# An LSTM feeding a binarised feed-forward block: x Wx in the cell's layout, seeded into the gates' PSUM by ScalarE, the output gate in its own bank

## The chip, the cores and the metric

The kernel runs on one core of one Trainium2 chip. Time is device microseconds for one execution. The times before are 329.32, 329.71 and 330.16 us (median 329.71). Names used below: PE is TensorE (matmuls), DVE is VectorE, ACT is ScalarE, POOL is GpSimd, SP is SyncE, which only issues DMAs here. SBUF is the on-chip memory, PSUM the accumulator memory that PE writes, made of eight banks.

## The reference

For a batch of N = 32 sequences of T = 64 steps and width D = 256:

```python
xW = einsum('ntd,dg->ntg', x, Wx) + b            # Wx: 256 x 1024 (4 gates of 256)
def step(h, c, xw_t):                            # 64 times, each needs the last h
    a = xw_t + h @ Wh                            # Wh: 256 x 1024
    i, f, o = sigmoid(a[:, :256]), sigmoid(a[:, 256:512]), sigmoid(a[:, 512:768])
    g = tanh(a[:, 768:])
    c = f * c + i * g
    h = o * tanh(c)
# feed-forward on all h, with weights of +1/-1 from boolean matrices
y = concat([h, -h]); y = relu(s0 * (y @ k0)) * 2     # 512 -> 1024
y = relu(s1 * (y @ k1)) * 2                          # 1024 -> 1024
out = x + s2 * (y @ k2)                              # 1024 -> 256
```

All is fp32. The recurrence is serial over 64 steps; the feed-forward part (FFN below) can start on the first sixteen steps once they exist.

## The kernel before, in words

**Layout.** The cell works on 128 partitions that hold four quarters q of the hidden width, 32 batch rows each: partition q*32+n, free dimension 64 columns per gate. A step's gates are 256 columns there. `gates_from_h` (L275) makes them with 2 x 4 fp32 matmuls, stationary h transposed (32 columns) and moving Wh (256 columns); each of the four q writes its own 32 partitions, so four matmuls run side by side in four column groups of PE. An fp32 matmul appears as two matmul records in the trace, hence 16 per step.

**The cell.** `cell_step`: DVE adds the x part out of SBUF (`a`, L287), ACT takes the sigmoid of three gates (`sig`, L292) and the tanh of the fourth (`cand`, L294), DVE forms `kept` (L298), `new` (L300) and `c` (L302), ACT takes `th` = tanh(c) (L304), DVE forms `h` (L306) and transposes it into `hist` (L311), from which the next step's matmuls read. Each engine works its instructions strictly in the order in which the program issues them.

**x Wx.** `turn_x` (L202) transposes x on DVE. `x_block` computes blocks of 16 steps with Wx stationary (32 columns at a time) and x moving (8 steps x 32 rows = 256 columns), L219. The result has gates on partitions and must be turned: ACT evicts it with the bias (`xb`, L241) and DVE transposes it (`xg`, L238). Block 0 is computed whole before step 0.

**FFN.** After every four steps `split_h` makes `hhi` and `hlo` (L324, L325) out of hist, a high and a low part of h. `ffn_block` works on blocks of 16 steps: layer 0 (L377), layer 1 (L406), layer 2 (L391), matmuls of 128 x 128 weights and 512 columns, each layer's result evicted as a high part by ACT (L330) and a low part by DVE (L331). A block has 192 such matmuls.

**Order.** All engines' orders are written by hand. The program emits, for each step t: the gates' matmuls, the cell, then a "chore" (one piece of the FFN's weights: `make_w0` L179/L180, `make_w1` L185, `make_w2` L189), then PE filler: so many pieces of x Wx (steps 0 to 16) or of the FFN (12 matmuls per step from step 17) that PE has work while the cell runs. The 192 matmuls of the last FFN block and the rest of the third follow after step 63.

**Loads.** x (L80) and the weights come by DMA. SP issues most: x's first block and Wx (L107, L117), Wh (L120), x's second block, the booleans k0 (L136, used by `make_w0` in steps 0 to 3) and k1, k2 (`load_bits`). ACT issues a share of the first ones, POOL the bias, the initial h and the scales. The eight hardware DMA semaphores are used in turn, so an issue waits for the transfer that was issued eight before it.

Of the kernel before, what the change touches and what calls it, by code (L numbers as in the profile page):

```python
# [36 lines left out]
def lstm_ffn(ctx: ExitStack, tc: tile.TileContext, x, cond, wx_d, wh_d, b_d, k0_d, k1_d, k2_d, s0_d, s1_d, s2_d, out):  # L38
# [10 lines left out]
    NM = G // P  # L49
# [4 lines left out]
    PER_STEP = 12  # L54
    LAG = SB + 1
# [4 lines left out]
    gpool = ctx.enter_context(tc.tile_pool(name="xg", bufs=NB))  # L60
# [4 lines left out]
    ps_g = ctx.enter_context(tc.tile_pool(name="ps_g", bufs=2, space=PSUM))  # L65
# [10 lines left out]
    def load_x(i, half, engines):  # L76
        t = xq[i, half] = xpool.tile([P, SB // 2, HQ], F32, tag="x", name=f"x{i}_{half}")
        t0 = i * SB + half * (SB // 2)
        for q in range(NQ):
            engines[q % len(engines)].dma_start(  # L80
                out=t[q * N : (q + 1) * N], in_=x[:, t0 : t0 + SB // 2, ts(q, HQ)]
            )


    small = const.tile([P, 96], F32, name="small")
    b_raw, bias = small[:, :32], small[:, 32:64]
    nc.vector.memset(b_raw, 0.0)
    wh = const.tile([P, 2, G], F32, name="wh")
    w0 = const.tile([P, 2, F0], F32R, name="w0")
# [8 lines left out]
    wx_rows = wx_d.rearrange("(q b j) g -> q j b g", q=NQ, b=2)  # L98
    wx = [act([P, 2, H], F32, f"wx{g}") for g in range(4)]

# [3 lines left out]
    load_x(0, 0, [nc.sync, nc.scalar])  # L104
    for q in range(NQ):
        engine = (nc.sync, nc.scalar)[q % 2]
        engine.dma_start(out=rows(wx[0], q), in_=wx_rows[q, :, :, :H])  # L107
    load_x(0, 1, [nc.sync, nc.scalar])
# [3 lines left out]
    b_rows = b_d.rearrange("(g q b j) -> q g b j", g=4, q=NQ, b=2)  # L112
    for q in range(NQ):
        nc.gpsimd.dma_start(out=b_raw[q * 32 : q * 32 + NM], in_=b_rows[q])
    for g in range(1, 4):
        for q in range(NQ):
            nc.sync.dma_start(out=rows(wx[g], q), in_=wx_rows[q, :, :, ts(g, H)])  # L117
    wh_rows = wh_d.rearrange("(q b j) g -> q j b g", q=NQ, b=2)
    for q in range(NQ):
        nc.sync.dma_start(out=rows(wh, q), in_=wh_rows[q])  # L120
# [55 lines left out]
    def make_w0(k, half):  # L176
# [3 lines left out]
        nc.vector.scalar_tensor_tensor(  # L180
# [19 lines left out]
    def turn_x(i, half):  # L200
        full = act([P, SB // 2, 2, N], F32, f"xT{i}_{half}")
        nc.vector.transpose(  # L202
            full.rearrange("p t b n -> p (t b n)"), xq[i, half].rearrange("p t j -> p (t j)")
        )
        xT[i, half] = full

    xg = {}

    def x_block(i):
        xg[i] = gpool.tile([P, SB, G // NQ], F32, tag="xg", name=f"xg{i}")  # L210

        for m0, side in ((0, 2), *((m, 1) for m in range(2, NM))) if i == 0 else ((m, 1) for m in range(NM)):
            ps = [ps_f.tile([P, 2, SB // 2, N], F32, tag="pf", name=f"px{i}_{m0 + j}") for j in range(side)]
            for half in range(2):
                for j in range(side):
                    g, b = divmod(m0 + j, 2)
                    for k in range(2):
                        for q in range(NQ):
                            nc.tensor.matmul(  # L219
                                ps[j][q * 32 : (q + 1) * 32, half],  # L220
                                wx[g][:, k, ts(2 * q + b, 32)],
                                xT[i, half][:, :, k, :],
                                start=(k == 0),
                                stop=(k == 1),
                                skip_group_check=True,
                            )
                        if k == 0:
                            yield 2
                    if half:
                        finish_x(i, m0 + j, ps[j])  # L230
                    yield 2

    def finish_x(i, m, p):
        out_t = xg[i]
        tmp = act([P, TB], F32, f"xb{i}_{m}")

        def turn(out_t=out_t, m=m, tmp=tmp):
            nc.vector.transpose(out_t[:, :, ts(m, 32)], tmp.rearrange("p (t n) -> p t n", n=N))  # L238

        def add_bias(m=m, p=p, tmp=tmp, turn=turn):  # L240
            nc.scalar.activation(  # L241
                tmp, p.rearrange("p h t n -> p (h t n)"), AF.Identity, bias=bias[:, m : m + 1]
            )
            on_vector(turn)

        on_scalar(add_bias)

    vector_queue, scalar_queue = deque(), deque()  # L250
    late = [False]

    def on_vector(f):
        vector_queue.append(f)

    def on_scalar(f):
        if late[0]:
            scalar_queue.append(f)
        else:
            f()  # L260

    def flush_vector(n=None):
        while vector_queue and n != 0:
            vector_queue.popleft()()
            n = None if n is None else n - 1


    wh_q = wh.rearrange("p k (g q j) -> p k q g j", g=4, q=NQ)
    hist, hparts = {}, {}
# [15 lines left out]
    def cell_step(t, g, c):  # L285
# [9 lines left out]
        while scalar_queue:  # L295
            scalar_queue.popleft()()
# [151 lines left out]
    n = 0  # L448
# [84 lines left out]
```

## Time and profile before

| What | us |
|---|---|
| Median of three runs | 329.71 |
| Profiled execution, its own time | 329.05 |
| Its span, first to last instruction | 327.2 |
| First gates (step 0) begin | 20.7 |
| Gates of step 2 begin | 29.52 |
| Gates of step 17 begin | 86.82 |
| Gates of step 63 begin | 270.14 |
| Last FFN block begins | 277.50 |
| Last matmul begins | 320.93 |

The span is the time between the first and the last instruction; 1.85 us of the execution lie around it. "Busy" is time in which an engine has an instruction in work; a matmul's end is modelled, so starts are the better guide on PE. In a row of the timeline the columns are start, duration, engine, line, operation, output<-inputs, shape, count, and in brackets the idle time before and what ended it. In the waits, the columns are total us, times, longest us.

### The profile page before, as it was taken

Reading aid. Unit: us, or ns where it says so; the run is one execution under the profiler, and the core shown is the slowest. Engines: PE = TensorE matmul, PEld = TensorE weight load, DVE = VectorE, ACT = ScalarE, POOL = GpSimd, SP = SyncE. Lnnn points to the kernel's source line nnn. Section 1 sums busy time; section 2 is a strip of 40 time slices with the busy share of each in tenths; the row PEclk is TensorE's granted clock in tenths of the full one; section 3 lists DMA queues with packets and bytes.
Section 4 is the critical chain, followed back from the end, with each engine's and each line's share of the span. In section 5 each row is a group of like instructions: output and inputs, shape, how many; then the busy total and the mean of one; then the engine's idle time right before and its main releaser. Section 6 shows DMA issues by size and latency. Waiting matters only on the chain.

```text
span 327.2 us, 7012 instructions
## 1 busy us (share of the span) xinstructions
PE 312.0 (95%) x2825; PEld 207.3 (63%) x2825; DVE 174.5 (53%) x538; ACT 125.5 (38%) x324; POOL 9.0 (3%) x27
## 2 busy tenths in 40 slices
PE   7987898999999999999999999999999999999992
PEld 3645555656666666666666666666666666888881
DVE  2357766665685445446856454568564444811104
ACT  1434566756653523234523232335232322511111
POOL 6200000000000000000000000000000000000001
PEclk9999999999999999999999999999999999999997
DMA  5765200104100000000010300000110000130002
GB/s 135 181 141 144 54 19 18 34 18 109 42 2 0 3 0 0 2 2 1 0 34 8 90 1 2 0 3 0 32 34 0 2 0 3 47 81 2 0 0 65
DMA packets 30864, 10.72 MB, mean 33 GB/s; under 512 B 28008, under 2 KB 30568, under 8 KB 30832
## 3 DMA queue, kind: packets, MB, share of 16 engines
q1 hardware_dynamic: 28224, 9.58, 12.4%
q10 hardware_dynamic: 2336, 0.66, 0.9%
q8 instruction: 22, 0.36, 0.5%
q0 software_dynamic: 272, 0.04, 0.1%
q14 instruction: 10, 0.08, 0.1%
HBM read 8.16 MB, written 2.10 MB: 31 GB/s over the span
## 4 chain that ended last, share of the span: by engine, by line
PE 79%; DVE 7%; DMA 5%; ACT 3%; SPq 2%; issue 2%; ACTq 0%; DVEq 0%
PE p L406 38%; PE gates L275 18%; PE p L377 10%; PE po L391 9%; PE px L219 5%; DMA x<-in_x_dram 2%; DVE xg L238 2%; DMA wh<-in_L_cond_Wh_dram 2%; SPq L117 2%; DVE a L287 1%; DMA wx<-in_L_cond_Wx_dram 1%; ACT xb L241 1%; ACT th L304 1%; DVE xT L202 1%; DVE h L306 1%
## 5 line engine op out<-in xcount | busy, mean ns | idle before, releaser
L275 PE MATMUL gates<-wh,hist 128*32 128x256 f32 x1008 | 67.5, 385 | 6.5 <-DVE hist L311 6.0
L292 ACT ACTIVATE sig<-a 128x192 f32<-128x192 f32 x64 | 23.4, 365 | 98.1 <-DVE a L287 98.1
L219 PE MATMUL px<-xT,wx 128*32 128x256 f32 x1024 | 59.3, 379 | 0.5 <-DVE xT L202 0.5
L287 DVE TENSOR_TENSOR a<-gates,xg 128x256 f32<-128x256 f32 x64 | 27.1, 423 | 55.7 <-PE gates L275 55.4
L275 PEld LDWEIGHTS gates<-wh,hist 128*32 128x32 f32 x1008 | 27.6, 109 | 40.6 <-issue 23.3
L219 PEld LDWEIGHTS px<-xT,wx 128*32 128x32 f32 x1024 | 37.8, 110 | 18.8 <-DVE xT L202 1.8
L304 ACT ACTIVATE th<-c 128x64 f32<-128x64 f32 x64 | 16.4, 257 | 35.9 <-DVE c L302 35.7
L306 DVE TENSOR_TENSOR h<-sig,th 128x64 f32<-128x64 f32 x64 | 14.4, 225 | 24.7 <-ACT th L304 24.7
L377 PE MATMUL p<-hhi,w 128*128 128x512 f32 x64 | 26.1, 408 | 0.0
L377 PE MATMUL p<-hlo,w 128*128 128x512 f32 x64 | 25.2, 393 | 0.0
L241 ACT ACTIVATE xb<-px,small 128x512 f32<-128x512 f32 x32 | 21.6, 674 | 9.1 <-PE px L219 9.0
L238 DVE STREAM_TRANSPOSE xg<-xb 128x512 f32<-128x512 f32 x32 | 22.1, 692 | 4.0 <-ACT xb L241 3.9
L298 DVE TENSOR_TENSOR kept<-sig,c 128x64 f32<-128x64 f32 x63 | 13.2, 210 | 8.7 <-ACT sig L292 8.7
L311 DVE STREAM_TRANSPOSE hist<-h 128x64 f32<-128x64 f32 x64 | 15.7, 246 | 2.2
L377 PEld LDWEIGHTS p<-hhi,w 128*128 128x128 f32 x64 | 12.0, 187 | 6.1 <-issue 3.3
L302 DVE TENSOR_TENSOR c<-kept,new 128x64 f32<-128x64 f32 x64 | 14.4, 225 | 2.2
L294 ACT ACTIVATE cand<-a 128x64 f32<-128x64 f32 x64 | 15.4, 240 | 0.0
L300 DVE TENSOR_TENSOR new<-sig,cand 128x64 f32<-128x64 f32 x64 | 14.1, 221 | 0.0
L406 PE MATMUL p<-a_2h,w 128*128 128x512 f32 x32 | 13.9, 433 | 0.0
L377 PEld LDWEIGHTS p<-hlo,w 128*128 128x128 f32 x64 | 12.0, 188 | 2.4
L406 PE MATMUL p<-a_6h,w 128*128 128x512 f32 x32 | 13.5, 423 | 0.0
L406 PE MATMUL p<-a_4h,w 128*128 128x512 f32 x32 | 13.2, 414 | 0.0
(119 smaller groups left out, 485.6 us busy)
## 6 DMA issues: line engine op xcount, KB each, us to landing
x<-in_x_dram SPq DMA_DIRECT2D x60, 64.0 KB, 2.7
out_dram<-o SPq DMA_DIRECT2D x28, 64.0 KB, 1.8
bits<-in_L_ffn_k_dram SPq DMA_DIRECT2D x10, 128.0 KB, 2.6
wh<-in_L_cond_Wh_dram SPq DMA_DIRECT2D x4, 256.0 KB, 4.3
wx<-in_L_cond_Wx_dram SPq DMA_DIRECT2D x14, 64.0 KB, 2.7
k<-in_L_ffn_k_dram SPq DMA_DIRECT2D x8, 64.0 KB, 1.9
x<-in_x_dram ACTq DMA_DIRECT2D x4, 64.0 KB, 2.6
out_dram<-o ACTq DMA_DIRECT2D x4, 64.0 KB, 2.0
```

The costliest lines, as they stand in the source:

```text
L219: nc.tensor.matmul(ps[j][q * 32 : (q + 1) * 32, half], wx[g][:, k, ts(2 * q + b, 32)], xT[i, half][:, :, k, :], start=(k == 0), stop=(k == 1),
L238: nc.vector.transpose(out_t[:, :, ts(m, 32)], tmp.rearrange("p (t n) -> p t n", n=N))
L241: nc.scalar.activation(tmp, p.rearrange("p h t n -> p (h t n)"), AF.Identity, bias=bias[:, m : m + 1])
L275: nc.tensor.matmul(g[q * N : (q + 1) * N], hT[:, k, :], wh_q[:, k, q], start=(k == 0), stop=(k == 1), skip_group_check=True,)
L287: nc.vector.tensor_tensor(a.rearrange("p g j -> p (g j)"), g.rearrange("p g j -> p (g j)"), xg[t // SB][:, t % SB, :], ALU.add)
L292: nc.scalar.activation(sig, a[:, 0:3, :], AF.Sigmoid)
L304: nc.scalar.activation(th, c, AF.Tanh)
L306: nc.vector.tensor_mul(h, sig[:, 2, :], th)
L311: nc.vector.transpose(hT, h.rearrange("p (b j) -> p b j", b=2))
L377: nc.tensor.matmul(p, w0[:, k, ts(m, P)], a[:, k, :], start=(n == 0), stop=(n == 3))
L391: nc.tensor.matmul(po[m], w2[:, m, k], a1[k][n], start=(k == 0 and n == 0), stop=(k == FC1 - 1 and n == 1))
L406: nc.tensor.matmul(p1[m], w1[:, k, ts(m, P)], a0[k][n], start=(k == 0 and n == 0), stop=(k == FC0 - 1 and n == 1),)
```

## The change

1. **x Wx in the cell's layout.** `x_part` takes x of one step as the stationary operand (32 columns) and Wx as the moving one (256 columns, four gates of the quarter q), so that the product stands on partitions as the gates do. Two steps share a PSUM bank. DVE evicts a bank with the bias added (`evict_x`, 128 x 512); the transposes of the result (L238) and ACT's evictions (L241) are gone. The bias is loaded replicated over the batch rows.
2. **Seeding.** After `th` of step t, ACT copies the x part of step t+1 out of SBUF into the gates' PSUM; the h matmuls add to it (`start=False`). The addition `a` on DVE is gone, and the sigmoids and tanh read PSUM.
3. **Gate order and banks.** The gates stand as g, i, f in one bank (192 columns) and o in another (64 columns). The h matmuls do the first bank, then the second: 8 matmuls of 192 columns and 8 of 64 per step instead of 8 of 256. `sig` is now a sigmoid of i and f, then `cand`, then a sigmoid of o.
4. **Order.** 10 steps of x Wx are done before step 0 (before: 16), the first 8 of them in two halves of the gates. Steps 0 to 20 share PE with the rest of x Wx, steps 21 to 63 with the first three FFN blocks (576 matmuls; before: 564 from step 17). Low parts of FFN evictions are emitted on DVE right behind ACT's. The DVE half of `make_w0` follows the step's x Wx pieces.
5. **Loads.** Wx and Wh come gate by gate, on the SP and ACT queues in turn (before: after the first Wx gate and x block, on SP alone). x's third block is loaded before step 0.

```diff
-    PER_STEP = 12
-    LAG = SB + 1
+    GATES = (3, 0, 1, 2)
+    AHEAD = 10
+    X_STEPS = 21
...
+    load_x(0, 0, [nc.sync, nc.scalar], slice(0, SB // 4))
+    load_gates(wx, wx_d, (2, 3), [nc.sync, nc.scalar])
+    load_x(0, 0, [nc.sync, nc.scalar], slice(SB // 4, SB // 2))
...
+    for q in range(NQ):
+        nc.gpsimd.dma_start(out=rows(bias, q)[:, 1:], in_=b_rows[q].partition_broadcast(N))
+    nc.gpsimd.tensor_copy(bias[:, 0], bias[:, 4])
+    for slot in range(2):
+        load_gates(wx, wx_d, (slot,), [nc.sync, nc.scalar])
     load_x(0, 1, [nc.sync, nc.scalar])
-    for g in range(1, 4):
-        for q in range(NQ):
-            nc.sync.dma_start(out=rows(wx[g], q), in_=wx_rows[q, :, :, ts(g, H)])
-    for q in range(NQ):
-        nc.sync.dma_start(out=rows(wh, q), in_=wh_rows[q])
+    load_gates(wh, wh_d, (0,), [nc.sync, nc.scalar])
+    load_gates(wh, wh_d, (1, 2, 3), [nc.sync, nc.scalar])
...
+    def x_part(p, t, k, slots, start):
+        i, s = divmod(t, SB // 2)
+        for q in range(NQ):
+            nc.tensor.matmul(
+                p[q * N : (q + 1) * N, t % 2, slots],
+                xT[i // 2, i % 2][:, s, k, :],
+                wx_q[:, k, q, slots],
+                start=start, stop=False, skip_group_check=True,
+            )
+    def evict_x(p, t):
+        xg[t] = gpool.tile([P, 2, 4 * HQ], F32, tag="xg", name=f"xg{t}")
+        b = bias[:, :4].rearrange("p g j -> p (g j)").unsqueeze(1).to_broadcast([P, 2, 4 * HQ])
+        nc.vector.tensor_tensor(xg[t], p.rearrange("p t g j -> p t (g j)"), b, ALU.add)
+    def x_products(t0, t1):
+        for t in range(t0, t1, 2):
+            p = x_bank(t)
+            for s in range(2):
+                for k in range(2):
+                    x_part(p, t + s, k, slice(0, 4), s == 0 and k == 0)
+                    if s == 1 and k == 1:
+                        evict_x(p, t)
+                        half, left = divmod(t + 2, SB // 2)
+                        if left == SB // 4 and half + 1 < 2 * NB:
+                            turn_x(*divmod(half + 1, 2))
+                            if half + 5 < 2 * NB:
+                                load_x(*divmod(half + 5, 2), [nc.sync])
+                    yield 2
...
+    gates = [ps_g.tile([P, n, HQ], F32, tag=f"gates{n}", name=f"gates{n}") for n in (3, 1)]
     def gates_from_h(t, hT):
-        g = ps_g.tile([P, 4, HQ], F32, tag="gates", name=f"gates{t}")
-        for k in range(2):
-            for q in range(NQ):
-                nc.tensor.matmul(g[q * N : (q + 1) * N], hT[:, k, :], wh_q[:, k, q],
-                                 start=(k == 0), stop=(k == 1), skip_group_check=True)
+        for g, slots in zip(gates, (slice(0, 3), slice(3, 4))):
+            for k in range(2):
+                for q in range(NQ):
+                    nc.tensor.matmul(g[q * N : (q + 1) * N], hT[:, k, :], wh_q[:, k, q, slots],
+                                     start=False, stop=(k == 1), skip_group_check=True)
+    def gates_from_x(t):
+        x_t = xg[t // 2 * 2][:, t % 2].rearrange("p (g j) -> p g j", g=4)
+        nc.scalar.copy(gates[0], x_t[:, :3])
+        nc.scalar.copy(gates[1], x_t[:, 3:])
-    def cell_step(t, g, c):
-        nc.vector.tensor_tensor(a..., g..., xg[t // SB][:, t % SB, :], ALU.add)
-        nc.scalar.activation(sig, a[:, 0:3, :], AF.Sigmoid)
-        nc.scalar.activation(cand, a[:, 3, :], AF.Tanh)
+    def cell_step(t, c):
+        nc.scalar.activation(sig[:, 0:2, :], gates[0][:, 1:3], AF.Sigmoid)
+        nc.scalar.activation(cand, gates[0][:, 0], AF.Tanh)
+        nc.scalar.activation(sig[:, 2, :], gates[1][:, 0], AF.Sigmoid)
...
         nc.vector.transpose(hT, h.rearrange("p (b j) -> p b j", b=2))
+        if t + 1 < T:
+            gates_from_x(t + 1)
...
+    for slots in (slice(2, 4), slice(0, 2)):
+        for t in range(SB // 2):
+            for k in range(2):
+                x_part(banks[t // 2], t, k, slots, slots.start == 2 and t % 2 == 0 and k == 0)
+            if slots.start == 0 and t % 2:
+                evict_x(banks[t // 2], t - 1)
...
+    work = x_products(AHEAD, T)
     for t in range(T):
-        g = gates_from_h(t, hT)
-        c, hT = cell_step(t, g, c)
+        gates_from_h(t, hT)
+        c, hT = cell_step(t, c)
+        later = chores.popleft()() if chores else None
+        if t == X_STEPS:
+            work, done = ffn(), 0
+        goal = (t + 1) * total_x // X_STEPS if t < X_STEPS else (t + 1 - X_STEPS) * total_ffn // (T - X_STEPS)
         while done < goal:
             done += next(work)
+        if callable(later):
+            later()
         if t % SH == SH - 1:
             split_h(t // SH)
```

## The prediction

> **What bounds the kernel now.** I read the busy table and its slices first, then busy time by stage, then the waits of the recurrent stage, and then one step of each stage in the timeline.
>
> ```profile
> PE 312.0 (95%) x2825; PEld 207.3 (63%) x2825; DVE 174.5 (53%) x538; ACT 125.5 (38%) x324; POOL 9.0 (3%) x27
> PEclk9999999999999999999999999999999999999997
> ```
>
> TensorE (PE) is busy for 95% and its clock is full, so time is either PE work or one of PE's few gaps. The busy time of three stretches tells where the gaps are. Columns: stretch, its length, then PE, weight load, DVE, ACT and POOL busy with counts, clock, DMA share, GB/s.
>
> ```profile
> 2.00:20.70 18.70, 17.59 (x264) 9.11 (x262) 5.91 (x12) 6.88 (x10) 6.63 (x21) 1.00 0.76 171
> 20.70:86.80 66.10, 59.64 (x1040) 37.92 (x1041) 45.60 (x140) 39.54 (x92) 0.00 (x0) 1.00 0.26 62
> 86.80:270.10 183.30, 183.28 (x1288) 119.31 (x1288) 103.70 (x347) 66.90 (x201) 0.00 (x0) 1.00 0.04 10
> ```
>
> The first stretch is the start (products of 16 steps before the first gates at 20.7), the second the 17 steps that share PE with x Wx, the third the 47 steps that share it with the feed-forward part (FFN). The second idles PE for 6.5 us, the third for nothing. What PE waits for in the second, from the waits of that window:
>
> ```profile
> ACT sig L292 <- DVE a L287: 19.0, 17, 2.9
> PE gates L275 <- DVE hist L311: 6.0, 10, 1.3
> ```
>
> So there the recurrence itself, gates to hist, sets the pace. One step of it in the timeline:
>
> ```profile
> 64.34 1.07 PE L275 MATMUL gates<-wh,hist 128*32 128x256 f32 x16
> 65.20 2.80 PE L219 MATMUL px<-xT,wx 128*32 128x256 f32 x48
> ...
> 65.47 0.42 DVE L287 TENSOR_TENSOR a<-gates,xg 128x256 f32<-128x256 f32 x1 [0.68 <-PE gates L275]
> ...
> 65.99 0.36 ACT L292 ACTIVATE sig<-a 128x192 f32<-128x192 f32 x1 [0.62 <-DVE a L287]
> ...
> 66.44 0.18 DVE L298 TENSOR_TENSOR kept<-sig,c 128x64 f32<-128x64 f32 x1
> 66.54 0.22 DVE L300 TENSOR_TENSOR new<-sig,cand 128x64 f32<-128x64 f32 x1
> ...
> 67.11 0.26 ACT L304 ACTIVATE th<-c 128x64 f32<-128x64 f32 x1 [0.61 <-DVE c L302]
> ...
> 67.66 0.25 DVE L311 STREAM_TRANSPOSE hist<-h 128x64 f32<-128x64 f32 x1
> ...
> 68.05 0.42 PE L275 MATMUL gates<-wh,hist 128*32 128x256 f32 x4
> ```
>
> From gates to gates 3.71 us: 1.13 to `a`, 0.52 to `sig`, 0.55 to `new`, 1.51 to the next gates. PE needs less: 16 gate matmuls take 65.20 - 64.34 = 0.86 (53.7 ns each, streamed), 48 of px 2.58, together 3.44. In the FFN stretch it is the reverse:
>
> ```profile
> 135.93 0.40 PE L406 MATMUL p<-a_0l,w 128*128 128x512 f32 x1
> ...
> 138.26 0.39 PE L406 MATMUL p<-a_5l,w 128*128 128x512 f32 x1
> 138.57 1.07 PE L275 MATMUL gates<-wh,hist 128*32 128x256 f32 x16
> ```
>
> Ten FFN matmuls from 135.93 to 138.26 are 0.233 each; a step is 138.57 - 134.59 = 3.99, of which 12 x 0.233 = 2.79 are FFN and 1.19 gates with the switch to 32-column groups and back. The same chain of 3.7 us lies under it.
>
> **Part 1: the recurrence.** `a` on DVE goes; `sig` and `cand` read PSUM. They wait for the first bank only, three quarters of the stream: 1.13 - 0.22 = 0.91 after the gates begin (before: 1.65). `sig` now has 128 columns, about 0.31; `cand` starts 0.22 after it and takes 0.24, so `new` comes at 1.41, and the row's 1.51 follows: a chain of 2.92 instead of 3.71. The output gate's sigmoid (64 columns, 0.24) is ready by 1.13 + 0.24 or behind `cand`, at 1.6, before `th` at 1.98: hidden. The chain falls below PE's own work, so the x stage becomes PE-bound, and the FFN stretch, PE-bound already, gains nothing from it directly.
>
> Added waits: the gates now wait for two ScalarE copies. The nearest rows for them are `sig` at 192 columns (0.36) and `cand` at 64 (0.24). Queued behind `th`, the first can start 0.16 after it (as xb did, 67.27) and ends at 0.52; the second ends at 0.67. `h` and `hist` end 0.80 after `th` starts. They cover the copies by 0.13; without the cover a delay would go into the chain, whose slack is 0.12 in the x stage and 1.4 in the FFN one. Behind the copies on ACT stand the weight chores (0.71 and 1.23) and `hhi` (0.40): 2.5 + 1.23 + 0.40 = 4.1 after the gates, against the next `sig` due at 3.04 + 0.91 = 3.95; a tenth or two, in two steps.
>
> **Part 2: splitting the gates' matmuls.** 16 matmuls of 256 columns become 16 of 192 and 16 of 64. The columns streamed are the same: 16 x 40.3 + 16 x 13.4 ns = 0.86. What is unknown is the price of the short ones. The Trainium skill's page "TensorE: Matmul & The Clock Gate" (section "Wait — 56ns, not 53.3ns?") speaks against it: starts are never closer than about 25 ns however few the columns. By that the 64-column half costs 16 x 25 = 0.40 instead of 0.21, 0.19 more per step, 12 us over 64 steps, which makes the kernel slower. The trace's row differs in kind, because four column groups run side by side: in the 30 ns from 138.57 four gate matmuls start. A short fp32 matmul also occupies its group for 4 x 13.4 = 54 ns, longer than that floor, and the visible part of a first load is 24 ns (403 against 379 ns of duration in the gates' rows). Ends: 0 and 0.19; I take 0.03, near the row.
>
> **Part 3: x Wx.** Matmul count and columns stay (1024 of 256 in the whole kernel; the first eight steps in halves of 128, same stream). 32 ScalarE xb (0.67) and 32 DVE turns (0.69) go; 32 DVE evictions with the bias, 512 columns out of PSUM, come at about 0.68 (row of the FFN's a_l). ACT gains 64 x (0.36 + 0.24) of copies and 64 more sigmoids. None of it is on PE. PE's step in the x stage: 0.86 + 0.03 + 5 x 8 x 0.0537 = 3.04, or 3.47 in the three steps with six pieces. Steps 2 to 20: 16 x 3.04 + 3 x 3.47 = 59.05. DVE is first in, first out: after step 3's `hist` (2.80) stand two evictions, a turn of x, a w0 half and `hlo`, 2 x 0.68 + 0.70 + 0.74 + 0.42 = 3.2, to 6.0, while `kept` is due at 3.47 + 1.26 = 4.73; with smaller cases in four steps with a turn I add 1.7. Sum 60.75.
>
> **Part 4: the start.** Each DMA issue takes SP about 0.47 and waits for the transfer eight issues earlier. SP issues 20 loads before x's second block, then 14; ACT takes the rest. wh landed at 18.1 (four of 256 KB, 1.2 us apart); with both queues issuing I put it near 15, and PE's own work before the gates (8 halves twice, 6.9, two more steps, 1.7, waiting for half of wx at about 6 and the rest at about 9.5) also ends near 14.6. First gates: 15.3 instead of 20.7. But step 0 holds a chore: w0's first part on ACT and its second on DVE, ahead of `kept` of step 1, and both need k0:
>
> ```profile
> 10.53 2.64 SPq L120 DMA_DIRECT2D wh<-in_L_cond_Wh_dram  x4
> 13.21 5.26 SPq L80 DMA_DIRECT2D x<-in_x_dram  x8
> 18.51 4.92 SPq L136 DMA_DIRECT2D k<-in_L_ffn_k_dram  x8
> ```
>
> Its last landing was near 25.0 (issued at 23.0, 1.9 to land), just before it was used at 26.34. In the new start it would be used at 19. Six issues fewer on SP bring it 6 x 0.47 = 2.8 forward, to 22.2; at wh's rate, the 14 x 256 KB up to k0's end, counted from 2.5 us, take 16.8 and end at 19.3; no gain leaves 25.0. I take 21.6, near the issue-bound end. This is what is late next: DVE ends the w0 half at 22.35, and `kept` to the next gates is 68.05 - 66.44 = 1.61, so the gates of step 2 start at 23.95 (before 29.52), whatever PE did earlier.
>
> **Sum.** Gates of step 21: 23.95 + 60.75 = 84.7. FFN steps: 576 matmuls in 43 steps are 13.4, so 3.99 + 1.4 x 0.233 + 0.03 = 4.345; 42 of them bring the gates of step 63 to 267.2. Before, those were at 270.14 and the last FFN block began at 277.50, with 23 matmuls between; now 13 or 14 stand there: 4.35 + 0.4 for a wait on the last eviction as now, so it begins at 271.95, 5.55 earlier. The rest (192 matmuls, outputs) is unchanged. Span 327.2 - 5.55 = 321.65, its execution 329.05 - 5.55 = 323.5, and since the median shown is 0.66 above that execution, 324.2.
>
> **Rivals.** (a) *The start gains nothing*: k0 lands at 25.0 as now, gates of step 2 at 27.35: 3.4 less, 327.6. For it: DMA is busy 76% in that stretch. Against: the second issuing queue.
> (b) *Short matmuls pay a floor* (the other side): 0.19 instead of 0.03 in each of 64 PE-bound steps is 10 more, 334. It decides from 0.03 + 5.55/64 = 0.12 per step. For it: the rule; against: four starts in 30 ns.
> (c) *The chain isn't shortened*: copies or PSUM reads run late and the x stage keeps a 3.4 us pace, 19 x 0.25 = 4.8 back: 329. For it: only 0.13 of cover; against: the rows.
> (d) *More*: k0 comes at wh's rate, 2.3 earlier, and half of the DVE queueing is absorbed: 321.
>
> **How the numbers follow.** Forecast 0.60 (own range 322 to 326.5), (a) 0.14, (b) 0.13, (c) 0.07, (d) 0.06. Within 0.3%, about 1 us, is what a measurement of this kernel can't tell from no change: 0.05, nearly all from (c). Faster: 0.60 + 0.14 + 0.06 + 0.02 = 0.82; slower 0.13. The range goes from 320, inside (d), to 329, which takes in (a) and most of (c) and leaves (b) out.
>
> **What would show it.** Gates of step 0 near 15.3, a long wait of step 1's `kept` or of w0 on k0's transfer, gates of step 2 near 24; steps of about 3.05 after step 4 with PE without gaps; gates of step 21 near 84.7; FFN steps of 4.35. A gates run over 1.1 us from first start to the next matmul would prove (b); PE waiting for ACT copies, (c).

## The result, and the profile after

| Kernel | Median of its runs, us | Ratio to the kernel before | 95% interval |
|---|---|---|---|
| Before (runs beside it) | 329.51 (328.10 to 330.16) | 1 | |
| Changed | 324.85 (324.65 to 325.26) | 0.9866 | 0.9832 to 0.9900 |

The forecast was 324.2. The profiled execution of the changed kernel took 325.26, its span is 323.5 (before: 329.05 and 327.2). The total was right, but by luck: two of its terms were wrong by 3 to 5 us in opposite directions, so I go through the stages. First the busy table of the page and its clock row (PEclk, the share of TensorE's full clock that was granted, in tenths).

```profile
PE 309.4 (96%) x3979; PEld 236.8 (73%) x3979; DVE 154.0 (48%) x473; ACT 131.0 (41%) x484; POOL 9.2 (3%) x28
PEclk9997999999999999999999999999999999999998
```

PE is still the busiest engine. What is new is the 7 in the fourth slice of the clock row (24 to 32 us): PE was granted less than its full clock there, which the kernel before showed in its last slice only. The same by stage, cut at the first gates, the gates of step 2, of step 21 and of step 63 (columns as in the prediction: stretch, its length, busy time of PE, weight load, DVE, ACT and POOL, clock, DMA share, GB/s):

```profile
2.00:17.57 15.57, 14.20 (x298) 10.77 (x297) 4.30 (x9) 1.95 (x4) 6.71 (x22) 1.00 0.77 193
17.57:28.50 10.93, 6.27 (x148) 4.71 (x145) 4.92 (x15) 3.17 (x14) 0.00 (x0) 0.97 0.52 135
28.50:89.48 60.98, 60.59 (x1392) 46.12 (x1396) 41.07 (x133) 36.70 (x134) 0.00 (x0) 0.98 0.21 50
89.48:268.69 179.21, 179.21 (x1910) 135.50 (x1903) 85.34 (x281) 77.04 (x309) 0.00 (x0) 1.00 0.04 10
```

From the gates of step 2 to those of step 21 PE now idles for 0.4 us; the stretch of x Wx before, which counted steps 0 and 1 in, idled it for 6.5. After the first gates, nearly all of PE's idle time is in the second row: two steps take 10.93 us, and PE works for 6.27 of them. The timeline of that stretch shows what it waits for (brackets: idle time before, and what ended it).

```profile
12.10 6.96 SPq L84 DMA_DIRECT2D x<-in_x_dram  x8
...
19.10 5.47 SPq L146 DMA_DIRECT2D k<-in_L_ffn_k_dram  x8
...
20.59 1.08 PE L269 MATMUL gates<-wh,hist 128*32 128x192 f32 x32
...
24.34 0.72 ACT L189 ACTIVATE w0t<-k,sgn 128x512 f32<-128x512 uint8 x1 [4.22 <-DMA k<-in_L_ffn_k_dram]
...
26.25 0.75 DVE L190 SCALAR_TENSOR_TENSOR w<-k,nsgn,w0t 128x512 fp32r<-128x512 uint8 x1 [4.51 <-DMA k<-in_L_ffn_k_dram]
...
26.92 0.22 DVE L290 TENSOR_TENSOR kept<-sig,c 128x64 f32<-128x64 f32 x1
...
28.50 1.93 PE L269 MATMUL gates<-wh,hist 128*32 128x192 f32 x32 [4.67 <-DVE hist L303]
```

Read it from below: the gates of step 2 waited 4.67 us for `hist`; `hist` comes from `kept` at 26.92, which stands on DVE behind the w0 half of step 0; that half waited 4.51 us for k0, whose issues on SP began only at 19.10. The chain of the prediction is there, 4.5 us later than forecast.

One step of the x stage, to be held against the one shown before:

```profile
52.12 1.08 PE L269 MATMUL gates<-wh,hist 128*32 128x192 f32 x32
...
53.09 0.28 ACT L286 ACTIVATE sig<-gates 128x128 f32<-128x128 f32 x1
53.27 0.22 ACT L287 ACTIVATE cand<-gates 128x64 f32<-128x64 f32 x1
53.37 0.23 ACT L288 ACTIVATE sig<-gates 128x64 f32<-128x64 f32 x1
...
53.55 0.22 DVE L292 TENSOR_TENSOR new<-sig,cand 128x64 f32<-128x64 f32 x1
...
54.47 0.20 ACT L281 COPY gates<-xg 128x64 f32<-128x64 f32 x1
54.60 0.24 DVE L303 STREAM_TRANSPOSE hist<-h 128x64 f32<-128x64 f32 x1
...
55.15 0.37 PE L269 MATMUL gates<-wh,hist 128*32 128x192 f32 x4
```

A step is 3.03 us. `hist` ends at 54.84, 2.72 after the gates began, and the next gates wait for nothing but PE's own work until 55.15. The last copy ends at 54.67, 0.17 before `hist`: hidden, as forecast (0.13). In the FFN stretch:

```profile
153.34 1.08 PE L269 MATMUL gates<-wh,hist 128*32 128x192 f32 x32
154.35 0.50 PE L371 MATMUL p<-hhi,w 128*128 128x512 f32 x1
...
157.43 0.39 PE L371 MATMUL p<-hlo,w 128*128 128x512 f32 x1
157.74 1.08 PE L269 MATMUL gates<-wh,hist 128*32 128x192 f32 x32
```

The run of 32 gate matmuls takes 1.01 us to the first FFN matmul; 16 of 256 columns took 1.00 by the same measure before (medians over the FFN steps). A step with 14 FFN matmuls is 4.41, one with 13 is 4.18.

Where the 1.85 us between the forecast span (321.65) and the measured one come from:

| Stretch | Forecast, us | Measured, us | Difference |
|---|---|---|---|
| To the gates of step 2 | 23.95 | 28.50 | +4.55 |
| Gates of step 2 to 21 | 60.75 | 60.98 | +0.23 |
| Gates of step 21 to 63 | 182.5 | 179.21 | -3.3 |
| Gates of step 63 to the last FFN block | 4.75 | 4.73 | 0 |
| From there to the end | 49.7 | 50.08 | +0.4 |

### The profile page after: what moved, and what is told of

The parts are those of the page before. It is cut to its first block, busy times and chain, and to the rows that moved or that the text cites. A ratio compares the mean times of both kernels' runs of the same rounds, so it can differ in the third digit from the quotient of the medians.

```text
span 323.5 us, 9433 instructions
## 1 busy us (share of the span) xinstructions
PE 309.4 (96%) x3979; PEld 236.8 (73%) x3979; DVE 154.0 (48%) x473; ACT 131.0 (41%) x484; POOL 9.2 (3%) x28
## 4 chain that ended last, share of the span: by engine, by line
PE 87%; DMA 5%; DVE 3%; SPq 3%; issue 1%; ACT 1%; DVEq 0%; ACTq 0%
PE p L399 38%; PE gates L269 19%; PE px L226 12%; PE p L371 10%; PE po L384 9%; DMA x<-in_x_dram 2%; DMA wh<-in_L_cond_Wh_dram 2%; SPq L146 1%; SPq L84 1%; DMA k<-in_L_ffn_k_dram 1%; DMA wx<-in_L_cond_Wx_dram 1%; DVE w L190 0%; DVE xg L241 0%; ACT th L296 0%; DVE hist L303 0%
## 5 line engine op out<-in xcount | busy, mean ns | idle before, releaser
L269 PEld LDWEIGHTS gates<-wh,hist 128*32 128x32 f32 x2016 | 54.6, 110 | 30.3 <-issue 14.1
L269 PE MATMUL gates<-wh,hist 128*32 128x192 f32 x2016 | 68.9, 277 | 5.0 <-DVE hist L303 5.0
L226 PE MATMUL px<-wx,xT 128*32 128x256 f32 (+1 forms) x1152 | 62.2, 366 | 1.4 <-DMA wx<-in_L_cond_Wx_dram 1.4
L226 PEld LDWEIGHTS px<-wx,xT 128*32 128x32 f32 x1152 | 41.3, 115 | 13.8 <-issue 2.7
L286 ACT ACTIVATE sig<-gates 128x128 f32<-128x128 f32 x64 | 17.7, 277 | 82.7 <-PE gates L269 82.5
L241 DVE TENSOR_TENSOR xg<-px,bias 128x512 f32<-128x512 f32 x32 | 21.2, 666 | 5.9 <-POOL nsgn L158 4.8
L280 ACT COPY gates<-xg 128x192 f32<-128x192 f32 x64 | 20.0, 313 | 8.4 <-DVE xg L241 8.4
L288 ACT ACTIVATE sig<-gates 128x64 f32<-128x64 f32 x64 | 14.8, 231 | 0.0
L287 ACT ACTIVATE cand<-gates 128x64 f32<-128x64 f32 x64 | 14.0, 218 | 0.1
L399 PE MATMUL p<-a_7h,w 128*128 128x512 f32 x32 | 13.0, 407 | 0.0
L281 ACT COPY gates<-xg 128x64 f32<-128x64 f32 x64 | 13.0, 203 | 0.0
```

What stands on the lines that cost most here:

```text
L226: nc.tensor.matmul(p[q * N : (q + 1) * N, t % 2, slots], xT[i // 2, i % 2][:, s, k, :], wx_q[:, k, q, slots], start=start, stop=False, ski ...
L241: nc.vector.tensor_tensor(xg[t], p.rearrange("p t g j -> p t (g j)"), b, ALU.add)
L269: nc.tensor.matmul(g[q * N : (q + 1) * N], hT[:, k, :], wh_q[:, k, q, slots], start=False, stop=(k == 1), skip_group_check=True,)
L280: nc.scalar.copy(gates[0], x_t[:, :3])
L286: nc.scalar.activation(sig[:, 0:2, :], gates[0][:, 1:3], AF.Sigmoid)
L288: nc.scalar.activation(sig[:, 2, :], gates[1][:, 0], AF.Sigmoid)
```

## The experiments

The theory is that of the prediction: the time is PE's work plus PE's gaps; the recurrence no longer sets the pace, and what remains is the wait of step 1 for k0. The rivals are that the seeding or the bank of its own did not matter, that short matmuls cost a floor, and that the start's loss lies in something other than k0's place. Each kernel below is the changed kernel with one edit, the last one with three; ratios are to the kernel before, run beside it on the same chip.

### 1. The chores begin in step 3

```diff
-        later = chores.popleft()() if chores else None
+        later = chores.popleft()() if chores and t >= 3 else None
```

> The changed kernel with the weight chores starting at step 3 instead of step 0; nothing else moves. Theory (k0's transfer, through make_w0's two halves ahead of sig and kept of step 1, pins the gates of step 2 at 28.5): those gates come 2 x 3.03 after the first ones, near 23.7, PE's 4.7 us gap there is gone, and about 0.5 comes back because step 6 now has a w0 half beside two evictions and a turn: 320.5 us. Rival (the start is limited by the transfers as such, x's second block or Wh): the gap stays in another place and the time is within 1 us of 324.9.

Measured: 321.76 us, ratio 0.9776 (0.9751 to 0.9802). Its busy time in the three steps from the first gates:

```profile
18.55:27.64 9.09, 9.09 (x216) 7.27 (x220) 5.35 (x19) 3.37 (x18) 0.00 (x0) 1.00 0.55 152
```

Steps 0 to 2 take 3.03 each, PE has no gap and full clock. The gates of step 3 come at 27.64 instead of 32.83; some is given back in step 7, which takes 3.71 because the last w0 half and a turn of x stand on DVE ahead of its `kept`, so the gates of step 21 come at 84.84 instead of 89.48. The stall of step 1 was the chore's, and moving one condition by three steps brings some 3 us. (The two profiled executions lie 4.7 apart; the changed kernel's, 325.26, is the longest of its four runs, and this one's, 320.56, the second shortest of its five.)

### 2. All four gates in one bank

One bank of 256 columns, h matmuls of 256 columns again, one copy of 256; the activations wait for the whole.

```diff
-    gates = [ps_g.tile([P, n, HQ], ...) for n in (3, 1)]
+    gates = [ps_g.tile([P, 4, HQ], ...)]
-        for g, slots in zip(gates, (slice(0, 3), slice(3, 4))):
+        for g, slots in zip(gates, (slice(0, 4),)):
...
-        nc.scalar.copy(gates[0], x_t[:, :3])
-        nc.scalar.copy(gates[1], x_t[:, 3:])
+        nc.scalar.copy(gates[0], x_t)
```

> The changed kernel with the four gates in one bank again: 8 matmuls of 256 columns, one copy of 256 columns by ScalarE, all three activations wait for the whole. Theory (the split takes a quarter of the stream, 0.22 us, off a chain of 2.86 that lies just below PE's 3.03, and costs PE about 0.01 per step): x steps of about 3.08 instead of 3.03, FFN steps the same, time 325 to 326. Rival (short matmuls cost PE, a floor of 25 ns each): FFN steps 0.1 to 0.19 shorter, time 315 to 320. Rival (the output gate's own bank is a large part of the gain): slower by more than 2 us, 327 or more.

Measured: 327.21 us, ratio 0.9944 (0.9922 to 0.9966). x steps are 3.09 instead of 3.03, FFN steps 4.21 and 4.44 instead of 4.18 and 4.41:

```profile
141.36 1.07 PE L269 MATMUL gates<-wh,hist 128*32 128x256 f32 x16
142.36 0.50 PE L383 MATMUL po<-a_4h,w 128*128 128x512 f32 x1
...
145.80 1.07 PE L269 MATMUL gates<-wh,hist 128*32 128x256 f32 x16
```

The gates' run is 1.00 here and 1.01 in the changed kernel, yet the step of 14 matmuls is 4.44 against 4.41: what follows the gates is slower after matmuls of 256 columns. By position, the medians of the distances between FFN matmuls are 0.240, 0.235, 0.233 and 0.236 us for the second to fifth here, the same as in the kernel before, and 0.236, 0.228, 0.233 and 0.231 in the changed one. So splitting the gates, which I priced as a cost, pays. The 0.03 in each of 42 FFN steps, 1.3 us, was not expected; with it the time reaches the number of the second rival, though the output gate's bank makes up less than half of the 2.4 us, as the next run shows.

### 3. One bank, but the matmuls stay split

As in 2, with the h matmuls cut into 64 columns (the output gate, first) and 192.

```diff
-        for g, slots in zip(gates, (slice(0, 4),)):
+        for g, slots in ((gates[0][:, 3:4], slice(3, 4)), (gates[0][:, 0:3], slice(0, 3))):
```

> All four gates in one bank and one copy of 256 columns, as in the run with one bank, but the h matmuls stay cut: first 64 columns for o, then 192 for the other three, so that the activations wait for the last pass as there. With one bank and 256-column matmuls the FFN matmuls after the gates stood 0.235 us apart against 0.228, and the FFN steps took 4.21 and 4.44 us against 4.18 and 4.41. Theory A (it is the width of the gates' matmuls): here 0.228 again, 4.18 and 4.41, time 325.5 to 326. Theory B (it is the bank, or what ACT and PE do in it): 0.235, 4.21 and 4.44, time near 327.2. If only the last pass before the FFN counts (192 columns here, 64 in the changed kernel, 256 in the run with one bank): a value between.

Measured: 325.51 us, ratio 0.9890 (0.9869 to 0.9911). FFN steps are 4.18 and 4.41 again and the distances are those of the changed kernel: theory A. It is the cut of the gates' matmuls and not the bank, nor the order of the passes; their width and their number change together, and these runs do not part them. The bank of its own is worth the rest: x steps are 3.10 here, against 3.03. There `sig` begins 1.20 us after the gates, behind the last pass, instead of 0.97, and 0.23 on a chain of 2.88 (measured under 6) is 3.11: the chain is the longer side again.

### 4. The addition back on DVE

The copies into PSUM are left out; DVE adds the x part out of PSUM (192 and 64 columns), the activations read SBUF. Matmuls, banks and order stay.

```diff
-                        start=False,
+                        start=(k == 0),
...
+        nc.vector.tensor_tensor(a[:, :3], gates[0], x_t[:, :3], ALU.add)
+        nc.vector.tensor_tensor(a[:, 3:], gates[1], x_t[:, 3:], ALU.add)
+        # sig, cand and sig read a; gates_from_x is not called
```

> The changed kernel without the seeding: the h matmuls start their banks, DVE adds the x part out of PSUM (192 columns, then 64), the activations read SBUF, ScalarE copies nothing. Layout, banks and order stay. Theory (the shorter chain is what makes the x stage PE-bound): the chain grows by 0.45 to about 3.3, x steps go from 3.03 to about 3.35, 18 steps make 5 to 6 us, FFN steps gain nothing or lose 0.05 each: 330 to 332 us. Rival (PE's work alone sets the time, and the layout is the gain): within 1 us of 324.9.

Measured: 334.10 us, ratio 1.0160 (1.0141 to 1.0179), 2 us above the expectation and slower than the kernel before. One of its x steps:

```profile
52.48 1.08 PE L269 MATMUL gates<-wh,hist 128*32 128x192 f32 x32 [0.74 <-DVE hist L307]
...
53.69 0.35 DVE L288 TENSOR_TENSOR a<-gates,xg 128x192 f32<-128x192 f32 x1
53.95 0.21 DVE L289 TENSOR_TENSOR a<-gates,xg 128x64 f32<-128x64 f32 x1
54.13 0.31 ACT L290 ACTIVATE sig<-a 128x128 f32<-128x128 f32 x1 [0.82 <-DVE a L288]
...
56.04 1.08 PE L269 MATMUL gates<-wh,hist 128*32 128x192 f32 x32 [0.33 <-DVE hist L307]
```

`sig` begins 1.65 after the gates instead of 0.97, the step is 3.56, and PE waits for `hist` in it. Eight of the nineteen steps from 2 to 20 take 3.29 to 3.30, near the 3.35 expected; the others take up to 4.78, which the expectation missed. The gates of step 21 come at 97.41 instead of 89.48. FFN steps stay at 4.18 and 4.41, so the faster FFN steps are not owed to the seeding. The seeding is what makes the x stage PE-bound; without it this kernel loses.

### 5. The gates' matmuls cut to 64 columns

```diff
-        for g, slots in zip(gates, (slice(0, 3), slice(3, 4))):
+        for s in range(4):
+            g, slots = (gates[0][:, s : s + 1], slice(s, s + 1)) if s < 3 else (gates[1], slice(3, 4))
```

> The h matmuls of the first bank are cut once more, so that a step's gates are 64 matmul records of 64 columns instead of 16 of 192 and 16 of 64; banks, copies and activations stay. Theory (a short matmul costs its columns: the trace shows 56 ns for a pass of four records of 64 columns and 162.5 ns for four of 192): 16 passes of 56 are 0.90 us instead of 0.87, the run of gates takes 1.03 us to the next FFN weight load, and the time is 324.9 + 64 x 0.022 = 326.3 us. Rival (records start no closer than 25 ns on average): 64 starts are 1.60 us, 0.73 more in each step, and the time is near 371 us. A middle case (the twice as many weight loads cost something that is not hidden): gates of 1.1 to 1.3 us, 330 to 345 us.

Measured: 328.95 us, ratio 1.0005 (0.9983 to 1.0028). In the forms of its groups (last columns: busy time, and mean ns of one matmul, which overlap):

```profile
L270 PE MATMUL gates<-wh,hist 128*32 128x64 f32 x4032 | 72.0, 222 | 3.6 <-DVE hist L304 3.4 <-issue 0.2
```

64 short matmuls a step, and the FFN steps are 4.20 and 4.43: 0.02 more each, as the theory had it. The floor of 25 ns per start would have added 0.73 to every step. So the rule that the prediction weighed does not hold for matmuls in four column groups. The rest of the 4 us is not in the FFN stretch: the gates of step 21 come at 93.05, 3.6 later than in the changed kernel. Of these, 1.6 stand before step 2 and have nothing to do with the matmuls: the w0 half that waits for k0 began at 27.80 instead of 26.25, in a kernel with the same loads, and the gates of step 2 follow it by 2.25 in both. The other 2.0 are in the x stage, where several steps take 0.1 to 0.4 more and the weight load is idle for an issue that the profile puts down to nothing. That part was not settled.

### 6. Other splits of x Wx: 17 steps, or 16 steps ahead

```diff
-    X_STEPS = 21
+    X_STEPS = 17
```

> The changed kernel with x Wx spread over 17 steps instead of 21, and the FFN over 47 instead of 43. Theory (both stages are PE-bound, so the division of filler among steps only moves work): x steps near 3.6, FFN steps near 4.0; four more gates stand among FFN matmuls, which costs 4 x 0.32, and the stalls of steps 1 and 3 are covered by a little more filler: 324 to 325.5 us. Rival (the division is itself a source of the gain): 327 us or more.

Measured: 322.87 us, ratio 0.9820 (0.9801 to 0.9839), better than expected. The gates of step 2 come at 27.59, 0.9 earlier, because the w0 half that waits for k0 began at 25.33, 0.9 earlier than in the changed kernel's profile; the loads are the same. What the split itself did: more pieces of x Wx fall into step 1, so PE ran out 1.5 later and idled 2.26 us, not 4.67, and its clock stayed full afterwards.

```diff
-    AHEAD = 10
+    AHEAD = 16
```

> 16 steps of x Wx before the first gates instead of 10, so that PE has its work behind it while step 1 waits for k0; the loads and the chores stay. Theory (the end is PE work plus PE's gaps, and step 1's gap of 4.7 us behind k0 is what the start lost): six more steps of products (6 x 0.86 = 5.2 us) stand before the first gates, which begin near 22.7; k0 still lands near 26.1, w0 of step 1 no longer waits for long, gates of step 2 near 28.9, but 24 pieces fewer are left for steps 2 to 20, which take 2.6 to 3.0 us instead of 3.03 to 3.6: 321.5 us. Rival 1 (the steps of the x stage are held by the recurrence's chain at 2.9 us or more, so that fewer pieces do not shorten them): gates of step 21 at 86 or later instead of 89.5, time 322 to 323.5. Rival 2 (the products before the first gates only push everything back): 326 to 330.

Measured: 320.22 us, ratio 0.9750 (0.9723 to 0.9777). The first gates come at 21.36, those of step 2 at 27.27, without any stall: PE had its work while k0 was under way. Steps of five pieces take 3.03, most steps of four 2.88:

```profile
30.45 1.08 PE L269 MATMUL gates<-wh,hist 128*32 128x192 f32 x32
...
32.93 0.24 DVE L303 STREAM_TRANSPOSE hist<-h 128x64 f32<-128x64 f32 x1
...
33.29 0.51 PEld L269 LDWEIGHTS gates<-wh,hist 128*32 128x32 f32 x16 [0.52 <-ACT gates L281]
```

With four pieces PE needs 0.87 + 4 x 0.43 = 2.6, so 2.88 is the recurrence's own pace: this run measures the chain that the prediction put at 2.92. (The last row names the second copy, L281, as what ended the wait; it ended at 33.00, and `hist`, which the weight load reads, at 33.17.)

### 7. Where k0's loads stand

First, k0's eight loads on SP ahead of x's second block instead of behind it.

```diff
-    load_x(1, 0, [nc.sync])
-    load_x(1, 1, [nc.sync])
...
         k0_bits.append(t)
+    load_x(1, 0, [nc.sync])
+    load_x(1, 1, [nc.sync])
```

> On SP k0's eight loads stand before x's second block instead of behind it. Theory (SP's place in the queue sets both): k0's issues run from 12.1 to about 19 and land by 20.7; x's second block takes k0's old place and its first half lands near 22.6; in step 0 DVE has the turn of that half ahead of w0 and of the kept of step 1, so the stall does not go but moves: turn to 23.3, w0 to 24.0, gates of step 2 near 25.7, time 324.9 - 2.8 = 322.1 us. Rival (bytes, not the place in the queue): k0 lands at 24 or later whatever its place, gates of step 2 near 28, time 324.5 to 326.

Measured: 322.70 us, ratio 0.9806 (0.9773 to 0.9839).

```profile
20.43 0.72 ACT L189 ACTIVATE w0t<-k,sgn 128x512 f32<-128x512 uint8 x1
...
23.60 0.71 DVE L213 STREAM_TRANSPOSE xT<-x 128x512 f32<-128x512 f32 x1 [2.11 <-DMA x<-in_x_dram]
24.24 0.71 DVE L190 SCALAR_TENSOR_TENSOR w<-k,nsgn,w0t 128x512 fp32r<-128x512 uint8 x1
...
26.45 1.93 PE L269 MATMUL gates<-wh,hist 128*32 128x192 f32 x32 [2.25 <-DVE hist L303]
```

k0 is there by 20.4, and now the turn of x's second block waits, on the same DVE, ahead of the same `kept`: the stall moves and halves, as the theory said (gates of step 2 at 26.45, expected 25.7). Of the six runs, three with a mean clock of 0.996 to 0.998 took 321.29 to 321.88 us, the other three, at 0.988 to 0.992, took 323.52 to 324.30; the profile is of the second kind, with half clock after the stall. Then, k0's loads issued by POOL:

```diff
-            nc.sync.dma_start(out=rows(t, q), in_=k0_rows[i, q])
+            nc.gpsimd.dma_start(out=rows(t, q), in_=k0_rows[i, q])
```

> k0's eight loads are issued by POOL behind its scales (free from 10.6 us on) instead of by SP behind x's second block; everything else stays. Theory (k0 came at 26.1 because SP reached it only at 19.1, its issues waiting for older transfers, not because the DMA engines were full): eight issues of 0.55 us from 10.6 end at 15, k0 lands by 20, Wh perhaps 1 us later than 17.4 since the bytes share the engines, first gates near 18.6, w0 no longer waits, gates of step 2 near 25, gates of step 21 near 86, time 324.9 - 3.5 = 321.4 us. Rival (the bytes bound it): k0 not before 24, or Wh pushed back by as much as k0 gains; gates of step 2 at 27.5 or later, time 324 to 326.

Measured: 322.65 us, ratio 0.9791 (0.9769 to 0.9813), between the two. POOL issued k0 from 10.35 to 15.4, and w0 no longer waited, which is the theory. Each of these transfers took 5.7 to 7.2 us to land instead of 1.8 to 3.6, the first gates came at 19.6 (expected 18.6, changed kernel 17.57), and those of step 2 at 27.59, which is the rival's number. But not for the rival's reason: PE had stood for 2.27 us before the first gates and worked at half clock from 20.02 to 23.44, and 1.7 of the 8.0 us from the first gates to those of step 2 are that. The two of its five runs with a mean clock of 0.998 took 320.87 and 321.47, the theory's 321.4. So the place in SP's queue set when k0 came. Whether the earlier k0 also held Wh up is not shown: in the eight kernels with the changed kernel's loads whose first gates waited for Wh, they came at 17.57 to 19.24.

### 8. Late chores, 12 steps ahead, 17 steps shared

```diff
-    AHEAD = 10
-    X_STEPS = 21
+    AHEAD = 12
+    X_STEPS = 17
...
-        later = chores.popleft()() if chores else None
+        later = chores.popleft()() if chores and t >= 3 else None
```

> The chores begin in step 3, 12 steps of x Wx stand before the first gates instead of 10, and the rest of x Wx shares 17 steps instead of 21. Theory (PE's work plus its gaps makes the time; with late chores alone PE still idled 2.0 us ahead of the first gates, waiting for Wh): two more steps of products (1.7 us) go into that gap, the first gates stay near 18.6, and the 17 steps in place of 21 change nothing by themselves: 321.8 - 1.7 = 320.1 us. Rival (the third half of x, which DVE now turns before the first gates, has not landed, or the early eviction stands ahead of step 0's kept): the first gates or those of step 1 come 1 to 2 us later and the time is 321.5 to 323.

Measured: 319.36 us, ratio 0.9710 (0.9695 to 0.9726), the lowest median of all. From the first gates to those of step 63:

```profile
18.21:28.60 10.39, 10.39 (x245) 8.23 (x240) 6.88 (x21) 3.37 (x18) 0.00 (x0) 1.00 0.53 143
28.60:77.95 49.35, 49.35 (x1141) 39.04 (x1136) 34.68 (x105) 30.27 (x102) 0.00 (x0) 1.00 0.20 47
77.95:262.30 184.35, 184.35 (x2039) 138.52 (x2032) 89.56 (x301) 83.03 (x336) 0.00 (x0) 1.00 0.06 13
```

PE has no gap in any of the three. What is left to gain is PE's work itself, and the start before 18.2.

## Why the prediction was right, point by point

Its mechanism was right in the main in parts 1 to 3 and wrong in part 4. That the total came within 0.7 us is luck: the start was forecast 4.55 us too early, the FFN steps 3.3 us too long.

**Part 1, the recurrence: right.** The chain was put at 2.92 and measured 2.88 where it sets the pace (AHEAD 16). The single terms: `sig` begins 0.97 after the gates (0.91 forecast), takes 0.28 (0.31), `hist` ends at 2.72. The copies take 0.31 and 0.20 (0.36 and 0.24 forecast). That the chain falls below PE's work is shown by the x stage, and its cause by the addition put back on DVE: 9 us.

**Part 2, the split: right to take it near nothing, and too high still.** 0.03 per step was taken, 0.01 is what the gates' run costs, against 0.19 by the floor. In four column groups the trace has four records of 64 columns in 56 ns, 14 each, not 25. Rival (b) falls with that, and rival (c) with the x steps of 3.03, in which PE waits for no copy. What the step missed is the other sign: the FFN matmuls behind the gates stand closer, 0.04 to 0.05 per step.

**Part 3, the x stage: right in its sum, 60.98 for 60.75, for a partly different reason.** The base is 16 x 3.03 + 3 x 3.46 = 58.86 (59.05 forecast). Queueing on DVE, for which 1.7 was taken, cost 0.8: 0.57 in step 4, the rest in steps 7, 8 and 18. The place was right: after step 3's `hist` two evictions, a turn, a w0 half and `hlo` do stand on DVE in step 4, and `kept` begins 2.01 us after the gates instead of 1.29. But the queue took 2.8 us from `hist` and not 3.2, and the other steps with a turn lost next to nothing. In its place stands a cost that I had not seen, 1.3 us in step 2, which took 4.33. The busy time around it in short stretches:

```profile
26.00:28.50 2.50, 0.00 (x0) 0.03 (x1) 1.86 (x7) 0.93 (x4) 0.00 (x0) 0.85 0.80 233
28.50:30.00 1.50, 1.50 (x25) 1.12 (x29) 1.12 (x2) 0.34 (x1) 0.00 (x0) 0.50 0.69 154
30.00:31.00 1.00, 1.00 (x26) 0.63 (x20) 0.53 (x3) 0.62 (x3) 0.00 (x0) 0.50 0.55 123
31.00:32.00 1.00, 1.00 (x24) 0.63 (x20) 0.64 (x4) 0.91 (x4) 0.00 (x0) 0.92 0.22 44
```

PE stood from 23.83 to 28.50. The trace's clock record gives half clock (0.50) from 27.75 to 31.16, which is some 2.7 us of PE's work: half of that, 1.3 us, is the cost. The stall behind k0 so cost 6.0 us, not 4.67, and late chores won both: from the first gates to those of step 3 they take 9.09 us instead of 15.26. The Trainium skill, page "TensorE: Matmul & The Clock Gate", section "Part 1: The HAM clock gate", has this rule: PE falls to half clock after an idle window of about 3.4 us and comes back after as long a busy one. The trace agrees in kind, but not on how long PE must stand (see the last section). The prediction read the full clock of the kernel before and did not ask what its own forecast would do to it: by its numbers step 1 lasted from 18.3 to 23.95, 2.6 us more than PE's work in it.

**Part 4, the start: wrong.** The step that failed is "Six issues fewer on SP bring it 6 x 0.47 = 2.8 forward, to 22.2", and with it the 21.6 taken. The place in the queue was the right cause (shown by k0 put first), the price of an issue was not. The six issues fewer are right, though SP had 22 loads ahead of x's second block and then 16, not 20 and 14. But SP reached that block at 12.10, 1.1 earlier than before and not 2.8, because its issues ahead of it waited 4.7 us in sum for older transfers, against 1.6 before; that these transfers were late because the loads of ACT's queue now shared the DMA engines with them fits and was not tested. The eight issues of that block then took 6.96 us (before: 5.26) and k0's 5.47 (before: 4.92). k0's last landing was near 26.1, a microsecond later than before. That microsecond is within the scatter: the w0 half, which starts 0.12 after k0's last landing, began at 24.90 to 27.80 in the seven kernels here that load k0 and use it as the changed one does (26.25). So in the start rival (a)'s mechanism held: k0 gained nothing, its gates of step 2 were 27.35 and the measured 28.50. That the time is not rival (a)'s 327.6 is owed to the FFN steps alone. The first gates, put at 15.3, came at 17.57: Wh's last loads were issued up to 12.5 and took 4.9 to 5.3 us to land, the last at 17.43, and PE's own work, its first passes at half pace (last section), ended no earlier. This cost nothing, because step 1 waited anyway.

**The FFN steps: mis-sized, 4.267 on average and not 4.345.** 1.4 more matmuls at 0.227 instead of 0.233, 0.01 instead of 0.03 for the split, and the closer FFN matmuls: together 0.078 in each of 42 steps, 3.3 us, which made up for most of the start.

## What to carry to other kernels

When a change brings the first steps forward, look for every instruction in them that needs a load which was not moved: in-order engines turn one early use of a late transfer into a stall of the whole chain, and using it three steps later cost a tenth of that here. Price a stall of TensorE with what follows it, the half clock, and not only with its length. A count of issues times the price of one does not tell when a transfer comes, if a second queue begins to fill the same engines. And a start that hangs on transfers needs more than one profile: with the same loads, k0's landing differed by 2.9 us from one profile to the next.

## What the runs showed of the hardware that was not expected

- *How long PE may stand.* Two gaps of equal length end differently: with 17 shared steps PE idled 2.26 us and kept its clock; with k0 first it idled 2.25 us and came back at half.

```profile
27.59:29.00 1.41, 1.41 (x44) 1.27 (x48) 1.41 (x3) 0.77 (x4) 0.00 (x0) 1.00 0.57 129
```

```profile
26.45:28.00 1.55, 1.55 (x29) 1.33 (x33) 1.12 (x2) 0.34 (x1) 0.00 (x0) 0.52 0.77 203
```

  The first row is the run with 17 steps, the second that with k0 first. The same section of the page calls the window free-running, which would let equal gaps end differently, and the clock records of the traces agree: in each of the twelve the granted clock changes only at multiples of 3.41 us from the record's first entry. Here is PE in the period of 3.41 us that holds the gap, or most of it, 17 steps first again:

```profile
23.83:27.24 3.41, 1.49 (x28) 0.78 (x20) 1.52 (x6) 1.32 (x8) 0.00 (x0) 1.00 0.70 207
```

```profile
23.10:26.51 3.41, 1.16 (x27) 0.56 (x20) 2.52 (x8) 1.00 (x4) 0.00 (x0) 1.00 0.72 190
```

  With 17 steps the gap runs past the end of its period, so that PE idles 1.92 us in it; with k0 first all 2.25 us lie in one. In the twelve traces, each of the 18 periods at full clock in which PE idled 1.95 us or more was followed by half clock, and none in which it idled 1.84 or less; from 1.87 to 1.94 both occur. So idle time counts by period, and somewhat more than half of one is enough: the idle window of 3.4 us that the page states need not be idle throughout, and the measurement decides. Where the periods fall differs from run to run, so one kernel can meet half clock in one run and not in the next, as the mean clocks of the runs with k0 first and with k0 by POOL suggest. In the middle of a kernel it lasted one period, 3.41 us, each time.

- *A slow stretch without its mark.* In the changed kernel's first 18 passes of x Wx (6.85 to 10.6), a pass of four matmuls of 128 columns took 213 ns, and 109 ns later; with late chores it was 109 from the start. The clock column says 1.00 for both. Compare the counts of PE:

```profile
6.85:9.00 2.15, 2.15 (x42) 2.15 (x46) 0.53 (x2) 0.00 (x0) 1.05 (x3) 1.00 0.62 175
```

```profile
6.91:9.00 2.09, 2.09 (x77) 2.09 (x81) 0.53 (x2) 0.00 (x0) 1.14 (x3) 1.00 0.67 192
```

  42 matmuls in 2.15 us (changed kernel) against 77 in 2.09 (late chores). The records explain it: the changed kernel's clock record has its first entry, full clock, at 10.68 us, late chores' at 4.45, and where there is no entry yet the column shows 1.00. In the four traces whose first entry comes at 9.78 to 10.68 the first passes take 213 ns; in the seven others of this layout, at 4.45 to 6.03, they take 109. So the stretch is half clock too. It was hidden behind the landing of Wh here.

- *Short matmuls and their neighbours.* Four matmuls of 64 columns in four column groups take 56 ns together. And FFN matmuls of 512 columns stand 0.228 to 0.233 us apart (third to fifth distance in a step) behind gates cut to 192 and 64 (or 64 alone), 0.233 to 0.236 behind gates of 256. The runs show with what it goes, not why.
